# Autocorrelation on Trainium2: last-position terms and lag weights on ScalarE and GpSimd, a third key/value bank

## The chip, the cores and the metric

The kernel runs on one core of a Trainium2 chip. A core has five engines that execute their own instruction streams in order and synchronise by semaphores: TensorE (PE in the profile: matrix products and transposes), VectorE (DVE), ScalarE (ACT: functions, copies, scaling), GpSimd (POOL: element-wise work here) and SyncE (SP), which in this kernel issues nearly all DMA transfers. Matrix products accumulate in PSUM[...]; everything else lives in SBUF. A separate weight-load stream of TensorE is shown as PEld.

The metric is the device time in microseconds (us) of one execution. All data are fp32.

## The reference, cut to what matters

`x` and `ctx` have 8 batches of 256 positions and 1024 channels. Four layers follow one another:

```python
x = x + tanh(g_xattn[0]) * autocorrelation(layernorm(x), ctx, ctx)
x = x + tanh(g_ffn[0])   * lora_ffn(layernorm(x))
x = x + tanh(g_xattn[1]) * attention(layernorm(x), ctx, ctx, mask)   # GQA, rope
x = x + tanh(g_ffn[1])   * fourier_ffn(layernorm(x))
```

The change lies in the first of them. Per batch and channel:

```python
corr   = ifft(fft(q) * conj(fft(k))).real        # over L = 256 positions
w, idx = top_k(corr, 11)                         # 11 lags per channel
w      = softmax(w)
out    = sum_i w[i] * v[min(idx[i] + pos, L - 1)]
```

A shift beyond the end repeats the last position of `v`. So the sum over shifts is a linear correlation of the lag weights with `v`, in which the last position of `ctx` plays a part of its own.

## The kernel before, in words

The batches go in two passes of four. A pass p runs `autocorrelation`, then `lora_ffn`, `attention` and `fourier_ffn`, each with pools of its own. The program order is not written out by hand: the tile framework's scheduler orders the instructions from its own cost model, and inserts the semaphores; each engine then executes its list in order. Pools give a tile a new buffer when an old one has been released, so a pool with one buffer makes the next writer wait for the last reader.

**A turn.** `autocorrelation` works in turns: a turn is one batch and one half (512 channels) of D, 8 turns a pass, 16 in all. Positions are paired front and back, so a tile is 128 positions by 512 channels. In a turn:

- `loads`: DMA of the context `cn` and of its last position, `end`, spread over all partitions.
- `sums` (L460 to L466): GpSimd makes `ke`, `ko`, `qe`, `qo` (sums and differences of the pairs; L460 is `ke`). VectorE then corrects `ke` by -2 `end` (L466).
- `turn`: transforms by matmuls (`dft`, L411, into the pool `ps_dft`, four banks); ScalarE copies `kr`, `kn`, `ki`, `vr`, `vi` from PSUM to SBUF (L484 to L496); VectorE adds 2S `end` to row 0 of `kr` (L498). `products` (L427) multiplies spectra: four VectorE multiplications that read PSUM, two GpSimd sums for `re`, `im`.
- `correlation`: matmuls into the one bank of `ps_cor`, copied to `cor` by ScalarE.
- `lags`, four times a turn, each on 128 channels by 256 lags: VectorE finds the 8 largest and then three more, marking them by NEG (`match_replace`, L581 writes `took`); ScalarE computes `ex = exp(cor - max)` (L577); VectorE multiplies the mask `took == NEG` by `ex` and sums it into `tot` (L583); VectorE inverts `tot` (L586) and ScalarE scales `w` by it (L587).
- GpSimd makes `both`, the sums and differences of `w`'s halves.
- The next turn works up `both` of the turn before: TensorE transposes it into `pt` (pool `ps_out`, one bank; ScalarE copies it to `wt`), transforms `wt`, `products` with the spectra of `k` and `v` give `er`, `ei`, `odr`, `odi`, and `back` transforms them to positions (`po`, in `ps_dft`) and adds them to `x` by `residual` (L370, VectorE).

**What runs between.** At marked places a turn calls `fill(n)`, which advances a generator by n steps. That generator is `keys_values`: projections of the context to keys and values by a scheme of seven products instead of eight (`SEVEN`), matmuls at L796 into banks of the pool `ps_kv`, two of them. `combine` evicts a bank (VectorE; L244 is one of its lines). A finished key goes through `rope` (L709 to L717: three VectorE multiplications, the first two at L714 and L715 into a temporary of one buffer, and one GpSimd addition, L717). Weight sums for values and context sums run on GpSimd, those for keys on VectorE. In pass 0 `fold_last_layer` follows, which folds the last layer's update into its weight: matmuls at L319 into `ps_kv`, VectorE additions at L326. The same `rope` is called for queries in `attention`.

**PSUM in this stage.** Four banks `dft`, one `cor` (one tile of 128 x 512), one `out`, two `kv`: eight.

Of the kernel before, what the change touches and what calls it, by code (L numbers as in the profile page):

```python
# [11 lines left out]
F32 = mybir.dt.float32  # L12
# [7 lines left out]
P = 128  # L20
# [26 lines left out]
def flamingo_kernel(ctx: ExitStack, tc: tile.TileContext, a: dict, out: bass.AP):  # L47
# [333 lines left out]


    def autocorrelation(p, xt, pools, beside, late):
        c1, w1, w2, ps_dft, ps_cor, ps_out = pools

        def fill(n):
            for _ in range(n):
# [60 lines left out]
        def sums(b, cols, cn, end):  # L448

            xn = big_tile("xn", [2, HALF], "xn")  # L450
            for i, lin in enumerate(norms[b]):
                nc.scalar.activation(
                    xn[:, i, :],
                    xt[b * 2 + i][:, cols],
                    AF.Identity,
                    bias=lin[:, 1:2],
                    scale=lin[:, 0:1],
                )
            qe, qo, ke, ko = one("qe"), one("qo"), one("ke"), one("ko")
            nc.gpsimd.tensor_add(ke, cn[:, 0, :], cn[:, 1, :])  # L460
            nc.gpsimd.tensor_sub(ko, cn[:, 0, :], cn[:, 1, :])
            nc.gpsimd.tensor_add(qe, xn[:, 0, :], xn[:, 1, :])
            nc.gpsimd.tensor_sub(qo, xn[:, 0, :], xn[:, 1, :])


            nc.vector.scalar_tensor_tensor(ke, end, -2.0, ke, ALU.mult, ALU.add)  # L466
            return b, cols, end, qe, qo, ke, ko


# [2 lines left out]
        def turn(this, before, coming):  # L472


            after = None
            if this:
                b, cols, end, qe, qo, ke, ko = this
                if coming:
                    coming = loads(coming)
                kr_ps, ki_ps = dft((KCE, ke)), dft((KSE, ko), (NYQ, ke))  # L480


                kr, ki, kn = sb("kr"), sb("ki"), sb("kn")
                nc.scalar.copy(kr, kr_ps)  # L484
                nc.scalar.copy(kn, kr_ps)
                nc.scalar.activation(ki, ki_ps, AF.Copy, scale=pair)
                nc.scalar.copy(kn[0:1, :], ki_ps[0:1, :])
                re, im = sb("re"), sb("im")
                products(spectrum((CE, SE), (qe, qo)), kr, ki, kn, re, im, False)
                fill(2)  # L490

            if this:
                vr_ps, vi_ps = dft((KCO, ko)), dft((KSO, ke))
                vr, vi = sb("vr"), sb("vi")
                nc.scalar.copy(vr, vr_ps)
                nc.scalar.copy(vi, vi_ps)  # L496

                nc.vector.scalar_tensor_tensor(  # L498
                    kr[0:1, :], end[0:1, :], 2.0 * S, kr[0:1, :], ALU.mult, ALU.add
                )  # L500
                fill((1 if p == 0 else 2) if before else 6 if p == 0 else 2)
            last = not this
            if before:
                if last:
                    fill(3)
                b_cols, b_tiles, (bkr, bki, bkn, bvr, bvi, both) = before

                wt = []
                for t in range(2):
                    pt = ps_out.tile([P, HALF], F32, tag="out", name="pt")  # L510
                    for c in range(4):
                        nc.tensor.transpose(pt[:, c * P : (c + 1) * P], both[:, t, c, :], ident)
                    wt.append(one(f"wt{t}"))
                    nc.scalar.copy(wt[t], pt)
                    fill(2 if last else 1)
                er, ei = sb("re"), sb("im")
                products(spectrum((CE, SE), wt), bkr, bki, bkn, er, ei, True)
                fill(2 if last else 1)
                odr, odi = one("odr"), one("odi")
                products(spectrum((CO, SO), wt[::-1]), bvr, bvi, bvr, odr, odi, True)  # L520
                fill(3 if last else 2)
            if this and coming:
                after = sums(*coming)

            def back(l):


                if before:
                    po = ps_dft.tile([P, HALF], F32, tag="dft", name="po")
                    for i, (k, sp) in enumerate(((0, er), (3, odi)) if l else ((1, ei), (2, odr))):  # L530
                        nc.tensor.matmul(po, inv2[:, k, :], sp, start=(i == 0), stop=(i == 1))  # L531
                    residual(b_tiles[0][:, b_cols], po, tg_x[0])
                    residual(b_tiles[1][:, b_cols], po, tg_x[0] if l else ntg_x[0])
                    fill(1 - l)

            if last:
                back(0)
                back(1)
                return None, None
            w = big_tile("xn", [4, S], "w")  # L540
            cor = correlation(re, im, 0)
            fill(1)
            back(0)
            cor += correlation(re, im, 2)
            for c in range(2):
                lags(w[:, c, :], cor[c])
            fill(1)
            back(1)
            for c in range(2, 4):
                lags(w[:, c, :], cor[c])  # L550
            both = big_tile("xn", [2, 4, P], "both")
            nc.gpsimd.tensor_add(both[:, 0], w[:, :, 0:P], w[:, :, P:S])
            nc.gpsimd.tensor_sub(both[:, 1], w[:, :, 0:P], w[:, :, P:S])
            return after, (cols, xt[b * 2 : b * 2 + 2], (kr, ki, kn, vr, vi, both))
# [12 lines left out]
        def lags(w, cor):  # L567


            top = w2.tile([P, 16], F32, tag="top", name="top", bufs=4)  # L570
            left = w2.tile([P, S], F32, tag="left", name="left", bufs=1)
            took = w2.tile([P, S], F32, tag="took", name="took", bufs=1)
            nc.vector.max(top[:, 0:8], cor)
            neg = w2.tile([P, 1], F32, tag="neg", name="neg", bufs=4)
            nc.vector.tensor_scalar(neg, top[:, 0:1], -1.0, None, ALU.mult)
            ex = w2.tile([P, S], F32, tag="ex", name="ex")
            nc.scalar.activation(ex, cor, AF.Exp, bias=neg)  # L577
            nc.vector.match_replace(left, top[:, 0:8], cor, NEG)
            nc.vector.max(top[:, 8:16], left)
            nc.vector.memset(top[:, 11:16], NEG)  # L580
            nc.vector.match_replace(took, top[:, 8:16], left, NEG)  # L581
            tot = w2.tile([P, 1], F32, tag="tot", name="tot", bufs=4)
            nc.vector.scalar_tensor_tensor(  # L583
                w, took, NEG, ex, ALU.is_equal, ALU.mult, accum_out=tot
            )
            nc.vector.reciprocal(tot, tot)  # L586
            nc.scalar.activation(w, w, AF.Copy, scale=tot)  # L587

# [117 lines left out]
                pass  # L706


    def rope(dst, x, cos, sin, pool):  # L709

        H = P // 2
        t = pool.tile([P, 2, S], F32, tag="rope", name="rope", bufs=1)
        tab = lambda t: t.unsqueeze(1).to_broadcast([t.shape[0], 2, S])
        nc.vector.tensor_mul(t[0:H], x[H:P], tab(sin[H:P, :]))  # L714
        nc.vector.tensor_mul(t[H:P], x[0:H], tab(sin[0:H, :]))  # L715
        nc.vector.tensor_mul(dst, x, tab(cos))  # L716
        nc.gpsimd.tensor_add(dst, dst, t)  # L717

    def keys_values(n, groups, pools, tab):
# [61 lines left out]
        for u in range(4):  # L781
# [4 lines left out]
            for r in SEVEN:  # L786
# [16 lines left out]
                if done:  # L803
                    c, (i, j) = done
                    if kind == "wk":
                        kT = out_tile(c)
                        rope(kT, c, tab[:, 0, :], tab[:, 1, :], w1)
                        place = kT_d.rearrange("(q l i) p t -> q i p l t", l=2, i=2)
                        nc.sync.dma_start(
                            place[i_u, i, :, :, t0 + j * S : t0 + (j + 1) * S], kT  # L810
                        )
                    else:
                        r0, c0 = t0 + j * S, i_u * HALF + i * S
                        nc.sync.dma_start(
                            v_d[r0 : r0 + S, c0 : c0 + S].rearrange("(t p) d -> p t d", p=P), c
                        )
# [33 lines left out]
    def attention(p, xt, gq, go, keep, norms, xops, ahead):  # L850
        with (
# [115 lines left out]
            def queries(step, qT):  # L967
# [3 lines left out]
                for r in SEVEN:  # L971
# [10 lines left out]
                    done = combine(r, ps, tiles, lambda tag: half(tag, 1), lambda ps: ps)  # L982
                    if done:
                        qT[done[1]] = half("qT", 7)
                        rope(qT[done[1]], done[0], tab_q[:, 0, :], tab_q[:, 1, :], w1)
                    yield

            def outputs(step, ops):
# [359 lines left out]
    for p in range(NPASS):  # L1348
        ga, gb = ("a", "b") if p % 2 == 0 else ("b", "a")
        xt = [xpool.tile([P, D], F32, tag="x", name="x") for t in range(TT)]  # L1350
        with (
# [4 lines left out]
            tc.tile_pool(name="kv2", bufs=2, reuse_waits="tile") as kw2,  # L1356
            tc.tile_pool(name="ac_dft", bufs=4, space=PSUM) as ps_dft,
            tc.tile_pool(name="ac_cor", bufs=1, space=PSUM) as ps_cor,
            tc.tile_pool(name="ac_out", bufs=1, space=PSUM) as ps_out,
            tc.tile_pool(name="kv_ps", bufs=2, space=PSUM) as ps_kv,  # L1360
        ):

            tab = kw1.tile([P, 2, S], F32, name="tab")
# [15 lines left out]
            if p == 0:  # L1379
# [2 lines left out]
            autocorrelation(  # L1382
                p,
                xt,
                (c1, aw1, aw2, ps_dft, ps_cor, ps_out),
                steps,
                lambda: load_x(range(2, TT)),
            )
# [183 lines left out]
```

## Time and profile before

| | |
|---|---|
| three runs, us | 3363.13, 3356.34, 3361.8 |
| median, us | 3361.8 |
| profiled execution, us | 3351.35 |
| its span, first to last instruction, us | 3349.6 |
| mean granted TensorE clock | 0.992 |
| L466 (VectorE, `ke`), 16 times, ns least / median / most | 671 / 1215 / 6620 |
| L498 (VectorE, row of `kr`), 16 times | 716 / 1362 / 1697 |
| L583 (VectorE, `w`), 64 times | 403 / 425 / 7043 |
| L577 (ScalarE, exp), 64 times | 491 / 507 / 513 |
| L460 (GpSimd, `ke`), 16 times | 1251 / 1268 / 1457 |

The profile is one execution, and its own time differs a little from the runs. The span is what the trace covers. A busy engine is one that executes something; an engine is idle because it waits for a semaphore or has nothing to issue, and the trace names the instruction that released it. TensorE's clock is granted in parts of full speed, and the tables by stretches of time give its mean. Where a table of stretches is shown, each row has the stretch, its length, and then for every engine the busy time and the number of instructions. In a timeline a row has the start, the duration, engine, line and operation, and in brackets how long the engine stood idle before it and which instruction released it.

### The profile page before, as it was taken

The page shows a single profiled execution, that of the slowest core. Times are in us where ns is not written, and L with a number is a line of the kernel's source. Part 1 is how long each engine was busy: PE and PEld are TensorE (multiplying, and loading weights), DVE is VectorE, ACT ScalarE, POOL GpSimd, SP SyncE. Part 2 cuts the span into 40 slices and gives each one's busy share as a digit, 9 for nine tenths or more (in the row PEclk, how much of TensorE's full clock was granted, in tenths as well). Part 3 has the DMA queues.
Part 4 walks back from the last instruction along what each step waited for, and adds up shares of the span by engine and source line. Part 5 has one row for each costly group of instructions (what it writes and reads, how often), then busy time and mean ns, then how long its engine had stood idle before and what let it go on. Part 6 is the DMA issues. An engine that isn't in the chain of part 4 may idle for free. (4 is left out here: it accounts for less than half of the span.)

```text
span 3349.6 us, 39704 instructions
## 1 busy us (share of the span) xinstructions
PE 3268.8 (98%) x13456; PEld 2408.0 (72%) x13456; DVE 2356.0 (70%) x4561; ACT 844.1 (25%) x2043; POOL 1513.2 (45%) x1437
## 2 busy tenths in 40 slices
PE   8999899999999999999999999999999999999999
PEld 6677456777777766775456677568888888888874
DVE  7787657877777776776647686457776777777773
ACT  1332111322232322222113332113222223222310
POOL 4554112334433475576344442113464554554672
PEclk9999999999999999999999999999999999999999
DMA  7534615333333454554353435043555455555551
GB/s 280 174 113 125 240 59 189 127 136 132 139 126 129 132 207 147 178 190 160 116 189 127 141 120 166 7 159 101 166 182 161 157 168 175 164 168 172 176 186 51
DMA packets 215784, 505.58 MB, mean 151 GB/s; under 512 B 25076, under 2 KB 102900, under 8 KB 215582
## 3 DMA queue, kind: packets, MB, share of 16 engines
q1 hardware_dynamic: 214430, 498.84, 44.2%
q0 software_dynamic: 1152, 4.19, 0.3%
q8 instruction: 108, 1.77, 0.2%
q14 instruction: 94, 0.77, 0.1%
HBM read 394.96 MB, written 108.00 MB: 150 GB/s over the span
## 5 line engine op out<-in xcount | busy, mean ns | idle before, releaser
L717 POOL TENSOR_TENSOR qT<-qT,rope 128x512 f32<-128x512 f32 x128 | 169.3, 1322 | 671.0 <-DVE qT L716 670.9
L975 PE MATMUL ps_q<-xn,wq 128*128 128x256 f32 x1920 | 428.9, 379 | 0.0
L975 PEld LDWEIGHTS ps_q<-xn,wq 128*128 128x128 f32 x1920 | 364.8, 190 | 50.5 <-PE po L677 0.5
L1140 DVE COPY_PREDICATED s<-keep,ps_s 128x512 f32<-128x512 uint8 x256 | 185.5, 728 | 217.9 <-PE ps_s L1131 181.0
L1145 ACT ACTIVATE s<-s,nmx 128x256 f32<-128x256 f32 x512 | 255.9, 500 | 282.7 <-DVE nmx L1142 281.6
L975 PE MATMUL ps_q<-xn_t,wq 128*128 128x256 f32 x1280 | 285.6, 379 | 0.0
L1154 DVE TENSOR_SCALAR s<-s,tot 128x256 f32<-128x256 f32 x512 | 266.1, 560 | 7.5
L1172 ACT COPY wT<-pt 128x512 f32<-128x512 f32 x256 | 138.2, 588 | 526.8 <-PE pt L1166 526.3
L975 PEld LDWEIGHTS ps_q<-xn_t,wq 128*128 128x128 f32 x1280 | 243.2, 190 | 33.1
L370 DVE SCALAR_TENSOR_TENSOR x<-po,tg,x 128x512 f32<-128x512 f32 x248 | 176.4, 743 | 128.0 <-PE po L1319 45.7
L1177 PE MATMUL av<-wT,v 128*128 128x256 f32 x1024 | 246.0, 382 | 1.7 <-ACT wT L1172 1.4
L1131 PE MATMUL ps_s<-kT,qT 128*128 128x256 f32 x1024 | 247.5, 379 | 0.0
L1177 PEld LDWEIGHTS av<-wT,v 128*128 128x128 f32 x1024 | 191.6, 190 | 55.9 <-issue 21.5
L1067 PE MATMUL po<-wo,oI 128*128 128x256 f32 x896 | 215.7, 381 | 1.9 <-issue 1.2
L1131 PEld LDWEIGHTS ps_s<-kT,qT 128*128 128x128 f32 x1024 | 191.8, 190 | 25.5 <-issue 0.7
L1004 PE MATMUL po<-wo,oT 128*128 128x512 f32 x448 | 201.9, 593 | 0.0
L1139 POOL MEMSET s<- 128x512 f32 x256 | 128.7, 528 | 131.9 <-PE pt L1166 124.4
L1067 PEld LDWEIGHTS po<-wo,oI 128*128 128x128 f32 x896 | 169.8, 191 | 25.6 <-issue 1.8
L1142 DVE TENSOR_REDUCE nmx<-s 128x2 f32<-128x512 f32 x256 | 174.4, 684 | 7.7
L1067 PE MATMUL po<-wo,oT 128*128 128x256 f32 x672 | 171.7, 382 | 6.4 <-PE pt L1166 4.0
L253 POOL TENSOR_TENSOR x<-x,part 128x512 f32<-128x512 f32 x48 | 63.4, 1320 | 233.4 <-ACT part L252 233.4
L1185 ACT COPY oT<-av 128x512 f32<-128x512 f32 x128 | 75.0, 586 | 370.1 <-PE av L1177 370.1
(290 smaller groups left out, 6361.4 us busy)
## 6 DMA issues: line engine op xcount, KB each, us to landing
wo<-wo_d SPq DMA_DIRECT2D x144, 512.0 KB, 4.8
wq<-in_wq_dram SPq DMA_DIRECT2D x104, 512.0 KB, 3.5
wq<-wq_d SPq DMA_DIRECT2D x96, 512.0 KB, 3.3
wo<-in_wo_dram SPq DMA_DIRECT2D x56, 512.0 KB, 3.4
wo_d<-fine_t SPq DMA_DIRECT2D x56, 512.0 KB, 3.4
wo<-wo_d SPq DMA_DIRECT2D x96, 256.0 KB, 3.4
w<-w_d SPq DMA_DIRECT2D x36, 512.0 KB, 5.4
wo<-in_wo_dram SPq DMA_DIRECT2D x72, 256.0 KB, 3.3
```

Source lines behind the costliest of these rows:

```text
L370: nc.vector.scalar_tensor_tensor(xs, ps, g, xs, ALU.mult, ALU.add)
L717: nc.gpsimd.tensor_add(dst, dst, t)
L975: nc.tensor.matmul(ps[:, l, :], wops[r][:, l, c, :], xo[r][:, c, :], start=(c == 0), stop=(c == KH - 1),)
L1004: nc.tensor.matmul(po, ops[r][:, h, t * P : (t + 1) * P], wops[r][:, h, :], start=(h == 0), stop=(h == 1),)
L1067: nc.tensor.matmul(po, left[r2][:, h, :], w[:, h, :], start=(h == 0), stop=(h == 1))
L1131: nc.tensor.matmul(ps[:, t, :], qT[i, n][:, l, t * P : (t + 1) * P], kT[:, n * S : (n + 1) * S], start=True, stop=True,)
L1140: nc.vector.copy_predicated(s, keep[b], ps)
L1142: nc.vector.tensor_reduce(nmx, s, AX.X, ALU.max, negate=True)
L1145: nc.scalar.activation(s[:, t, :], s[:, t, :], AF.Exp, bias=nmx[:, t : t + 1], accum_out=tot[:, t : t + 1],)
L1154: nc.vector.tensor_scalar(s[:, t, :], s[:, t, :], tot[:, t : t + 1], None, ALU.mult)
L1172: nc.scalar.copy(wT[i], pt)
L1177: nc.tensor.matmul(av[:, i, :], kv[step][1][:, n * 2 + c, :], wT[i][:, c, :], start=(c == 0), stop=(c == 1),)
```

## The change

1. The correction of `ke` goes from one VectorE instruction to a ScalarE scaling of `end` by -2, in place, and a GpSimd addition.
2. The correction of row 0 of `kr` goes from one VectorE instruction to a ScalarE scaling of the already scaled row (-S times -2 `end` is 2S `end`) into a new tile `back_end`, and a GpSimd addition on one partition.
3. In `lags`, the masked product with its sum is replaced. ScalarE exponentiates `took`, in which the chosen lags stand as NEG and become zero, and the 16 values of `top`, of which the last five are NEG, with their sum as `tot`. GpSimd subtracts: `w = ex - exp(took)`, which leaves the chosen lags. `took` gets two buffers instead of one (the pool's number).
4. `pt` moves to the pool `ps_dft`. The pool `ps_out` goes, and `ps_kv` has three banks instead of two.
5. `rope` takes the number of buffers of its temporary as an argument: two for keys, one, as before, for queries.

```diff
-        c1, w1, w2, ps_dft, ps_cor, ps_out = pools
+        c1, w1, w2, ps_dft, ps_cor = pools
...
-            nc.vector.scalar_tensor_tensor(ke, end, -2.0, ke, ALU.mult, ALU.add)
+            nc.scalar.activation(end, end, AF.Copy, scale=-2.0)
+            nc.gpsimd.tensor_add(ke, ke, end)
...
-                nc.vector.scalar_tensor_tensor(
-                    kr[0:1, :], end[0:1, :], 2.0 * S, kr[0:1, :], ALU.mult, ALU.add
-                )
+                back_end = one("back_end")
+                nc.scalar.activation(back_end[0:1, :], end[0:1, :], AF.Copy, scale=-1.0 * S)
+                nc.gpsimd.tensor_add(kr[0:1, :], kr[0:1, :], back_end[0:1, :])
...
-                    pt = ps_out.tile([P, HALF], F32, tag="out", name="pt")
+                    pt = ps_dft.tile([P, HALF], F32, tag="dft", name="pt")
...
-            took = w2.tile([P, S], F32, tag="took", name="took", bufs=1)
+            took = w2.tile([P, S], F32, tag="took", name="took")
...
             tot = w2.tile([P, 1], F32, tag="tot", name="tot", bufs=4)
-            nc.vector.scalar_tensor_tensor(
-                w, took, NEG, ex, ALU.is_equal, ALU.mult, accum_out=tot
-            )
+            nc.scalar.activation(took, took, AF.Exp, bias=neg)
+            nc.scalar.activation(top, top, AF.Exp, bias=neg, accum_out=tot)
+            nc.gpsimd.tensor_sub(w, ex, took)
             nc.vector.reciprocal(tot, tot)
             nc.scalar.activation(w, w, AF.Copy, scale=tot)
...
-    def rope(dst, x, cos, sin, pool):
+    def rope(dst, x, cos, sin, pool, bufs):
...
-        t = pool.tile([P, 2, S], F32, tag="rope", name="rope", bufs=1)
+        t = pool.tile([P, 2, S], F32, tag="rope", name="rope", bufs=bufs)
...
-                        rope(kT, c, tab[:, 0, :], tab[:, 1, :], w1)
+                        rope(kT, c, tab[:, 0, :], tab[:, 1, :], w1, 2)
...
-                        rope(qT[done[1]], done[0], tab_q[:, 0, :], tab_q[:, 1, :], w1)
+                        rope(qT[done[1]], done[0], tab_q[:, 0, :], tab_q[:, 1, :], w1, 1)
...
-            tc.tile_pool(name="ac_out", bufs=1, space=PSUM) as ps_out,
-            tc.tile_pool(name="kv_ps", bufs=2, space=PSUM) as ps_kv,
+            tc.tile_pool(name="kv_ps", bufs=3, space=PSUM) as ps_kv,
```

More of the change, by code (lines that the diff above doesn't have):

```diff
@@ L1384, in flamingo_kernel @@
                 xt,
-                (c1, aw1, aw2, ps_dft, ps_cor, ps_out),
+                (c1, aw1, aw2, ps_dft, ps_cor),
                 steps,
```

## The prediction

> **What bounds the kernel now.** First the page's busy times: TensorE (PE) is occupied 98% of the span. Then busy time by stage. The change lies in the two autocorrelation stages, 0 to 374 us and 1720 to 2080 us, and in the fold behind the first.
>
> ```profile
> span 3349.6 us, 39704 instructions
> PE 3268.8 (98%) x13456; PEld 2408.0 (72%) x13456; DVE 2356.0 (70%) x4561; ACT 844.1 (25%) x2043; POOL 1513.2 (45%) x1437
> ...
> 0.00:374.00 374.00, 352.80 (x1355) 256.18 (x1356) 274.52 (x667) 102.70 (x182) 181.02 (x149) 0.98 0.51 174
> 374.00:480.00 106.00, 95.05 (x327) 48.74 (x326) 75.02 (x170) 11.16 (x23) 10.79 (x8) 0.97 0.48 169
> 1720.00:2080.00 360.00, 341.34 (x1335) 250.53 (x1334) 255.99 (x629) 96.95 (x174) 164.56 (x129) 0.98 0.44 145
> ```
>
> The columns are length, then PE, weight loads, VectorE (DVE), ScalarE (ACT), GpSimd (POOL), clock, DMA. PE is the bound here too; only its idle time can be won: 21.2 us in the first stage, 18.7 in the second. Added to that is the time it runs at half clock after a long gap:
>
> ```profile
> 75.60:82.40 6.80, 4.75 (x11) 3.87 (x12) 5.20 (x11) 0.77 (x1) 6.37 (x5) 0.50 0.31 117
> 130.20:133.60 3.40, 3.40 (x7) 2.02 (x8) 3.26 (x11) 1.48 (x3) 0.37 (x1) 0.51 0.00 0
> 1737.90:1744.70 6.80, 5.69 (x14) 4.55 (x15) 4.68 (x12) 0.30 (x1) 1.27 (x1) 0.50 0.48 134
> 1789.10:1792.50 3.40, 3.40 (x7) 2.04 (x7) 2.01 (x4) 0.00 (x0) 2.34 (x3) 0.50 0.63 193
> 1908.60:1915.40 6.80, 2.90 (x7) 2.37 (x8) 6.80 (x8) 0.00 (x0) 2.59 (x3) 0.50 0.53 176
> ```
>
> Last, who makes PE wait: the source view of line 466, and the timeline around the longest gap.
>
> ```profile
> L466 DVE SCALAR_TENSOR_TENSOR ke<-end,ke x16: 671/1215/6620, 26.0 to 1987.1; 128x512 f32<-128x512 f32 x16
> ...
>   POOL ke L460: 66.1, 15
> ...
> 1904.62 6.62 DVE L466 SCALAR_TENSOR_TENSOR ke<-end,ke 128x512 f32<-128x512 f32 x1 [7.98 <-POOL ke L460]
> ...
> 1912.50 0.80 PE L796 MATMUL ps_k<-cx,wk 128*128 128x256 f32 x1 [6.35 <-DVE v L244]
> ...
> 114.37 7.04 DVE L583 SCALAR_TENSOR_TENSOR w<-took,ex 128x256 f32<-128x256 f32 x1
> ```
>
> VectorE stands at L466 for GpSimd's ke (66.1 us over 15 turns), then spends 6.62 us on an operation that costs 0.67 at best. The evictions of the key and value banks queue behind it, and PE, with two such banks, stops.
>
> **The change, part by part.** A turn is one (batch, half) step; there are 16, each with four lags.
>
> *VectorE loses* L466, L498 and L583. From their minima and excess over them: 16 x 0.67 + 13.6 = 24.3; 16 x 0.72 + 7.8 = 19.3; 64 x 0.40 + 9.5 = 35.3, and 64 accumulator reads of 0.083 = 5.3. Together 84 us, with 66 us of standing.
>
> *GpSimd gains* two additions a turn and one subtraction a lag. 128x512 costs 1.27 (L460), 128x256 0.73 (L1046); one row of 512 I take at 1.27 too, since time goes by row length (ScalarE's one-row copy L487 takes 0.56 against 0.59): 32 x 1.27 + 64 x 0.73 = 87 us. Its stages go from 345.6 to some 433 of 734 us: room on the mean, but it executes in order.
>
> *ScalarE gains*, per lag, exp of 128x256 (0.50, L577) and exp of 128x16 (0.30, L350's small row) with accumulator read (0.19, L1145); per turn the scaling (0.6 as L484) and a row (0.56): 64 x 0.99 + 16 x 1.16 = 82 us on 200 of 734. The order of instructions has 24 function-table loads before and after.
>
> *What is won on PE.* Gaps with this cause, each with the half clock behind it (half of the stretches above):
> - 73.2: 4.10 + 3.4. The rope at L714 waits 6.37 for L717's addition, which stands behind GpSimd's weight sums; the second rope buffer and third bank remove it.
> - 124.5: 5.02 + 1.7. The residual L370 is behind the 7.04 us L583.
> - 217.6 and 277.6: 1.1 + 0.7 (bank behind L466; residual late).
> - 1734.1 and 1784.0: 4.52 + 3.4 and 3.62 + 1.7, evictions behind L466.
> - 1822.4: 1.80, GpSimd's re behind ko; in the new order PE has other work there.
> - 1905.6: 6.35 + 3.4.
> Sum 40.8 us.
>
> *What the next thing in line takes back.* At 73.2 PE comes 7.5 us early to the key transform, 77.8 instead of 85.3. GpSimd ended ko at 80.3 and the new addition ends at 81.6, the rope addition now behind it: 3.8 back. At 124.5 ScalarE's multiplication by 1/tot must wait for GpSimd's subtraction, queued behind weight sums up to 118.65 for the first lag and 121.9 for the second. Behind it in ScalarE's order stand the second exp and the second cor copy (end 123.8 instead of 122.9). Through the lags the residual ends at 128.2 instead of 129.95: PE still waits 3.3 + 1.7, 5.0 back. At 1734.1 and 1784.0 I take back 1 each, for the later ke. At 1905.6, from both at 1895.4, GpSimd has some 19 operations to the end of odr, 1919.4; PE would need it at 1924.4 - 9.75 = 1914.6: 4.8, and some half clock, 5.8 back. Together 16.6; 24.2 us stay.
>
> *New waits.* A lag's end loses the VectorE product (0.43 + 0.08) and gets exp, exp-with-sum and subtraction; after the match_replace it is about 0.7 us later, and recip on VectorE now waits for ScalarE where it followed at once. Behind recip stand the next lags and the residuals that free PE's transform bank; in turns at 167, 203, 241, 314 and 1852 they end 0.4 to 1.0 us before PE needs them. I take 0.3 for 12 turns, 3.6. Where PE already waits for both without slack (353.5 and 2051.7) 1.1 each; in the turn at 152, two table loads of 1.28 now lie before the last exp: 0.7. Together 6.5. Nothing (a gain in VectorE time alone) would be below these; 3 us per turn above.
>
> *pt in the transform banks:* it follows the spectrum products; they end 1.7 to 5 us before pt in most turns: nothing, or 0.5 a turn if ScalarE's copies come late. *Loads:* as many as before; the end loads shift on SP by a few places among weights that no PE wait names. *Fold:* 14 products now come in a row; VectorE (0.6 per 128x512, by their starts) sets the pace. It reaches the last additions, which free the next stage's banks, at 401.5 instead of 403.65, and the weight loads behind them shift alike: 2.4 won.
>
> Net: 24.2 - 6.5 + 2.4 = 20 us. The profiled execution took 3351.35 (span 3349.6 and 1.75 around it) and becomes 3331; from the median of 3361.8, 3341.5.
>
> **Two rules weighed.** *Gap and clock.* The row: after gaps of 4.10, 4.52 and 6.35 us half clock held for 6.8 us, after 5.02 and 3.62 for 3.4. [...] I take the row. [...] Left are those reading PSUM (L370 0.74, L427 0.68) and one-input ones (L581 0.41, L348 0.67), which keep their durations beside a busy GpSimd: no charge.
>
> **Rivals.**
> 1. *Nearly all is kept*: ScalarE and GpSimd are prompt, so only the wait for ke at 73.2 comes back: 40.8 - 3.8 - 2 + 2.4 = 37; 3325. For it: ScalarE 27% busy, GpSimd idle some 10 us ahead of most both. Against: in-order queues.
> 2. *No change*: gaps move. New waits of 1.5 us a turn (24) eat the 24.2: 3360. For it: PE stands close behind the residuals.
> 3. *Slower: the lag loop VectorE, ScalarE, GpSimd.* ScalarE stands at L587's scaling for a subtraction; behind it wait the copies of kr and ki, so the products, so the banks. Price: 3 us in each of 16 turns, 48 us, less 26.6 won, plus half clock of 1.7 in a few: +25, 3387. It decides from 1.7 us a turn on. For it: in two turns GpSimd's sums stand in the way. Against: in the other turns GpSimd is idle then.
> 4. *VectorE was not the cause* and PE waits for the cor/lag chain itself[...]; 3352.
>
> **How the numbers follow.** Forecast 0.55, rival 1 0.10, rival 4 0.08, rival 2 0.13, rival 3 0.14. The runs before lie within 0.2%, 6.7 us: that is what a measurement tells from no change. Faster takes the forecast, 1 and 4, less 0.02 of tails: 0.71; same 0.14; slower 0.15. The likeliest one's own range is 3330 to 3354. The range takes in rivals 1 and 2 and the mild half of 3: 3322 to 3373; outside is about 0.15.
>
> **What would show it.** VectorE about 84 us less in all, POOL +87, ACT +80. In the stages PE idle from 40 to about 25. No PE wait over 4 us at 73, 1734 and 1784; one left of some 3 us near 124 on L370; near 1905 one on GpSimd's odr. If ScalarE's line 587 waits for POOL w by more than 2 us in most turns, rival 3 holds; if PE's idle time in the stages stays at 40, the cause was elsewhere.

## The result, and the profile after

The changed kernel takes 3386.68 us (median of 4 runs, 3383.54 to 3390.19); the kernel before, 3362.47. The ratio is 1.0082, 95% interval 1.0068 to 1.0096: slower by 24 us, where 20 us faster was forecast. The time lies above the range of the prediction.

The page of the changed kernel and its busy times in stretches of the two stages (second stage shifted, since it begins 15 us later; columns as in the prediction):

```profile
span 3384.8 us, 39881 instructions
PE 3278.7 (97%) x13456; PEld 2414.0 (71%) x13456; DVE 2292.9 (68%) x4401; ACT 905.2 (27%) x2267; POOL 1590.6 (47%) x1533
...
0.00:374.00 374.00, 351.19 (x1355) 255.34 (x1356) 242.17 (x587) 133.14 (x294) 220.29 (x197) 0.99 0.50 174
1735.00:2104.00 369.00, 333.81 (x1280) 243.53 (x1279) 213.25 (x540) 127.54 (x286) 199.80 (x175) 0.94 0.39 131
```

The work moved about as forecast: VectorE 63 us less, ScalarE 61 more, GpSimd 77 more. TensorE gained nothing: in the first stage its busy time is what it was, in the second it is idle for 35 us of 369, and its clock there is 0.94 instead of 0.98.

To place the loss I take the start times of six matmuls by their number in TensorE's order, which hardly differs between the kernels: the first, those numbered 1370 (in the fold), 1500 (in the next layer), 6340 (some 33 us ahead of the second stage), 7560 (near its end), and the last. Two executions were profiled of each kernel; the second of each is the control described with the experiments.

| us between these matmuls | before | before, again | after | after, again |
|---|---|---|---|---|
| first stage | 375.3 | 376.2 | 374.8 | 374.6 |
| fold and head of the next layer | 45.2 | 45.1 | 48.8 | 48.4 |
| attention and the last layer, first pass | 1260.4 | 1258.7 | 1272.1 | 1270.0 |
| second stage | 346.2 | 338.7 | 369.4 | 371.9 |
| rest | 1310.8 | 1308.9 | 1308.3 | 1311.4 |

On the mean of two, 28 us are lost in the second stage, 11.5 in attention, 3.4 in the fold; 1 is won in the first stage. That is 42 us and not 24, because the two profiled executions of the kernel before are faster than its medians (3351.35 and 3341.27 against 3362.47 and 3356.88): what its slower executions lose more no profile here shows, so the split holds for the profiled executions, the ratio for the time.

Who makes TensorE wait in the second stage of the changed kernel (the waits by engine and line: total, times, longest):

```profile
PE dft L411 <- ACT wt L515: 28.0, 4, 8.9
PE dft L411 <- ACT kn L486: 4.2, 1, 4.2
PE pt L513 <- POOL both L553: 1.8, 1, 1.8
```

None of the waits of the kernel before is there (1734, 1784, 1822, 1905; such numbers give, as in the prediction, the start of the last matmul ahead of a wait). A new one is: four times TensorE stands for ScalarE's copy of `pt`. The wait of 4.2 us for `kn` has the same origin: ScalarE has stood for a load until 1777.86, and the lag instructions behind it come ahead of the copy of `kn`. The timeline of one of the four, ScalarE first, then the DMA queue (SPq), GpSimd and TensorE:

```profile
1842.82 0.57 ACT L515 COPY wt<-pt 128x512 f32<-128x512 f32 x1
1851.36 0.63 ACT L466 ACTIVATE end<-end 128x512 f32<-128x512 f32 x1 [7.97 <-DMA end<-in_ctx_dram]
1851.89 0.57 ACT L515 COPY wt<-pt 128x512 f32<-128x512 f32 x1
...
1845.65 0.33 SPq L445 DMA_DIRECT2D end<-in_ctx_dram  x1
...
1844.36 1.27 POOL L467 TENSOR_TENSOR ke<-ke,end 128x512 f32<-128x512 f32 x1
...
1844.48 1.02 PE L411 MATMUL dft<-wt,mats 128*128 128x512 f32 x2
1852.52 2.08 PE L411 MATMUL dft<-wt,mats 128*128 128x512 f32 x2 [7.01 <-ACT wt L515]
```

Between its two copies of `pt` ScalarE scales `end` by -2, for the addition that comes two turns later, and stands 7.97 us for the load. The load is no sooner because `end` has two buffers: it is issued at 1845.65, when GpSimd's addition of two turns before (L467, to 1845.6) has released one. So the chain runs GpSimd's addition, load (5.3 us at the median), ScalarE's scaling, the copy behind it, TensorE. The source view of the load, before and after, says it in one line each. Before, nobody waits for it:

```profile
L445 SPq DMA_DIRECT2D end<-in_ctx_dram x16: 333/418/1108, 16.3 to 1948.8; - x16
...
who waited for it (us, times):
```

After, ScalarE does in 14 of 16 turns:

```profile
L445 SPq DMA_DIRECT2D end<-in_ctx_dram x16: 328/402/822, 16.9 to 1941.7; - x16
...
who waited for it (us, times):
  ACT end L466: 99.1, 14
```

With each of these five gaps comes a stretch at half clock, which begins while TensorE still stands; three of the five are longer than any row that the prediction took (stretches of the changed kernel; the clock is the third column from the end):

```profile
1783.10:1789.90 6.80, 5.03 (x8) 2.68 (x9) 5.56 (x21) 5.54 (x15) 2.73 (x3) 0.50 0.35 116
1800.10:1810.30 10.20, 5.96 (x11) 3.87 (x12) 1.29 (x2) 2.52 (x4) 3.86 (x4) 0.50 0.47 171
1847.90:1858.10 10.20, 5.58 (x11) 3.84 (x12) 1.29 (x2) 2.52 (x4) 2.74 (x3) 0.50 0.56 171
1895.70:1902.50 6.80, 3.31 (x6) 2.01 (x7) 1.20 (x2) 3.00 (x5) 0.42 (x1) 0.50 0.81 286
1943.50:1953.70 10.20, 5.76 (x11) 3.87 (x12) 1.29 (x2) 2.52 (x4) 5.63 (x5) 0.50 0.52 179
```

That is 44 us at half clock, in which TensorE is busy for 25.6. In the timeline above two matmuls of L411 take 2.08 us in such a stretch and 1.02 ahead of it, so by an estimate from these about half of the 25.6, 13 us, is lost beside the 32 us of waits.

Why only the second stage? ScalarE stands for the load in the first as well (44.4 us in 6 waits). What differs is the place of L466 in ScalarE's order. In the second stage it stands, in four turns, between the two copies of `pt`, as in the timeline above: L515, L466, L515. In the first stage it stands behind both copies of a turn, or ahead of the first turns. ScalarE stands 9.50 us there ahead of the scaling at 150.02, and TensorE runs on without a gap.

### The profile page after: what moved, and what is told of

The parts are those of the page before. It is cut to its first block, busy times and chain, and to the rows that moved or that the text cites. A ratio compares the mean times of both kernels' runs of the same rounds, so it can differ in the third digit from the quotient of the medians.

```text
span 3384.8 us, 39881 instructions
## 1 busy us (share of the span) xinstructions
PE 3278.7 (97%) x13456; PEld 2414.0 (71%) x13456; DVE 2292.9 (68%) x4401; ACT 905.2 (27%) x2267; POOL 1590.6 (47%) x1533
## 4 chain that ended last, share of the span: by engine, by line
PE 80%; DVE 6%; POOL 5%; DMA 3%; issue 2%; ACT 1%; SPq 0%; POOLq 0%; DVEq 0%; ACTq 0%
PE ps_q L977 22%; PE po L1069 9%; PE po L1006 9%; PE av L1179 6%; PE ps_s L1133 6%; PE po L670 6%; PE po L1321 5%; PE ps_k L798 3%; PE pt L1168 3%; PE dft L411 3%; PE ps_v L798 3%; DVE s L1156 1%; DMA end<-in_ctx_dram 1%; PE po L532 1%; PE pa L626 1%
## 5 line engine op out<-in xcount | busy, mean ns | idle before, releaser
L1156 DVE TENSOR_SCALAR s<-s,tot 128x256 f32<-128x256 f32 x512 | 272.2, 572 | 7.5
L1144 DVE TENSOR_REDUCE nmx<-s 128x2 f32<-128x512 f32 x256 | 174.5, 684 | 7.7
```

The source lines that it names most:

```text
L1144: nc.vector.tensor_reduce(nmx, s, AX.X, ALU.max, negate=True)
L1156: nc.vector.tensor_scalar(s[:, t, :], s[:, t, :], tot[:, t : t + 1], None, ALU.mult)
```

## Experiments

Theories: S, ScalarE stands in order for the load of `end`, and TensorE for what is queued behind; L, the lag loop over VectorE, ScalarE and GpSimd (the prediction's third rival); A, the loss comes from attention, where VectorE is held. Ratios are to the kernel before, on the same chip. Four columns give the profile's segments as above, and "held" counts the places in attention and the last layer of the first pass where VectorE's scaling of the weights (L1154 before, L1156 after) takes over 2.5 us instead of 0.35.

| | ratio, 95% interval | first stage | fold | attention, last layer | second stage | held |
|---|---|---|---|---|---|---|
| after | 1.0082 (1.0068 to 1.0096) | 374.8 | 48.8 | 1272.1 | 369.4 | 5 |
| L466 in program order | 0.9932 (0.9912 to 0.9953) | 376.7 | 48.6 | 1270.2 | 322.5 | 5 |
| L466 and L500 in program order | 0.9943 (0.9925 to 0.9962) | 377.3 | 50.1 | 1270.1 | 322.5 | 5 |
| after, lags on VectorE | 1.0044 (1.0028 to 1.0059) | 374.6 | 49.2 | 1270.1 | 365.0 | 5 |
| both in order, lags on VectorE | 0.9940 (0.9922 to 0.9957) | 372.8 | 50.9 | 1259.4 | 322.7 | 2 |
| after, `ke` and `kr` on VectorE | 0.9957 (0.9942 to 0.9973) | 377.1 | 49.7 | 1269.7 | 327.7 | 5 |
| before + `ke` | 1.0023 (1.0011 to 1.0035) | 376.5 | 45.1 | 1262.1 | 351.7 | 3 |
| before + `ke` in program order | 0.9951 (0.9931 to 0.9970) | 377.6 | 45.1 | 1265.8 | 324.8 | 4 |
| before + bank, rope buffers | 0.9941 (0.9924 to 0.9958) | 366.4 | 51.1 | 1267.4 | 327.4 | 5 |
| before + bank, rope, `ke` in order | 0.9940 (0.9925 to 0.9955) | 376.0 | 48.5 | 1269.5 | 322.7 | 5 |
| before + lags | 1.0018 (1.0006 to 1.0030) | 381.3 | 45.3 | 1262.3 | 338.5 | 3 |

**One scheduling edge.** The same instructions on the same engines; L466 may only not be issued ahead of what the program names before it on ScalarE, and comes to stand behind L452 of its own turn, starting 1.4 us after it in most turns, instead of as much as two turns ahead (the expectation says nearly one).

```diff
-            nc.scalar.activation(end, end, AF.Copy, scale=-2.0)
+            tc.keep_in_program_order(nc.scalar.activation(end, end, AF.Copy, scale=-2.0))
```

> The changed kernel with one scheduling edge more: ScalarE's scaling of end (L466) may not be issued ahead of what the program names before it on ScalarE, so it moves from nearly a turn early to behind the same turn's normalisation L452. Same instructions, same engines. Theory S (ScalarE stands in order for the end load, 99.1 us in 14 waits, and the copies wt of L515 queue behind it): the wait at L466 falls from 99 to under 15 us, the four TensorE waits for L515 in the second stage (28.0 us and their half clock) go, and the time falls by about 23 us to 3355 to 3370. Rival L (lag loop: ScalarE's L589 waits for GpSimd's subtraction): nothing changes, 3380 to 3390. Rival A (the loss lies in attention, where VectorE's L1156 is starved 8 us at a time, 11 of the 24 us): only what the phase gives, 3375 to 3395.

Measured: 3338.28 us, 48 less than the changed kernel, 0.68% faster than the kernel before. The source view of L466 and TensorE's longest waits in the second stage:

```profile
L466 ACT ACTIVATE end<-end x16: 612/614/633, 27.6 to 1981.3; 128x512 f32<-128x512 f32 x16
...
  DMA end<-in_ctx_dram: 8.6, 3
```

```profile
PE pt L513 <- POOL both L553: 1.8, 1, 1.8
PE ps_k L798 <- DVE x L370: 0.8, 1, 0.8
PE pt L365 <- DVE xn L355: 0.6, 1, 0.6
```

The wait for the load fell from 99.1 to 8.6 us, the four waits are gone, and the second stage is 46.9 us shorter; no other segment moved by more than 2. TensorE's order is the same in both kernels, matmul for matmul. This is what theory S forecast, at twice the price that was expected: the expectation counted back to the kernel before, but behind the wait lay the gain of the change, too. Theory A falls as the cause; the loss in attention stays all the same, 1270.2 us here, too.

**The second edge.** L500 held in the same way, `tc.keep_in_program_order(nc.scalar.activation(back_end ...))`. In the changed kernel it stands 41.7 us for GpSimd's L501.

> As the run with L466 held in program order, and the scaling of the row into back_end (L500) held as well, so it stands behind the copy of vi. Theory S: beside the wait for end, the 41.7 us that ScalarE stands at L500 for GpSimd's L501 go too; 0 to 8 us below the run with one edge, 3350 to 3365. Rival L: 3380 to 3390. Rival A: 3375 to 3395.

The ratios overlap, 0.9943 and 0.9932, and the second stage takes 322.5 in both. The expectation held that up to 8 us lay in the 41.7. This run cannot tell, since the first edge had removed them already: with L466 held alone, the scheduler places L500 directly behind it, and ScalarE does not stand at L500 at all. So the first edge took two waits of ScalarE away at once. Which of them counted is told by the timeline, in which TensorE is released by the copy behind L466, and by a pair of kernels without L500, the `ke` correction alone, further down.

**The lags.** In the changed kernel, `lags` as before:

```diff
-            nc.scalar.activation(took, took, AF.Exp, bias=neg)
-            nc.scalar.activation(top, top, AF.Exp, bias=neg, accum_out=tot)
-            nc.gpsimd.tensor_sub(w, ex, took)
+            nc.vector.scalar_tensor_tensor(
+                w, took, NEG, ex, ALU.is_equal, ALU.mult, accum_out=tot
+            )
```

> The changed kernel with the lags as before: VectorE's masked product with its sum is back, ScalarE's two exponentials and GpSimd's subtraction are out, took has one buffer. Theory S: ScalarE still stands at L466 for the end load, 80 to 100 us, TensorE still waits at L515 in the second stage; 3375 to 3392. Rival L: the loss is gone, 3340 to 3360.

It stays slower than before, with ScalarE standing 81.4 us for the load in 12 waits and TensorE 26.4 us for the copies. Theory L falls as the cause of the loss, though not wholly: the intervals of 1.0044 and 1.0082 do not overlap, so the lags part adds 0.4% here. How much of that comes by way of the load's wait, 81.4 us against 99.1, is not told apart. The same edit with both edges:

> The changed kernel with L466 and L500 held in program order and the lags back on VectorE with one buffer of took. It tells what the lags part is worth once ScalarE no longer stands for the load: 3338 to 3344 if it is worth nothing, 3345 to 3358 if VectorE's masked product costs TensorE its waits again (0.4 us in each of 64 lags and the held ones).

0.9940 against 0.9943: once the wait is gone, no worth of the lags part, for better or worse, can be told. Alone on the kernel before:

> The kernel before with the lags alone on ScalarE and GpSimd (two exponentials, the subtraction, two buffers of took). By the prediction's sum of new waits and of the 124.5 gap, between 6 us slower and 6 us faster; 3353 to 3368. Rival L (lag loop): 3375 or more. Places with 8 us of held VectorE in attention: 2 if the banks bring the others.

1.0018, slightly slower. The profile shows 5.5 us more in the first stage than the mean of the two of before, and in the second the time of the faster of the two profiles of before. In the first stage TensorE's wait at 174.9 for `both` is new (2.6 us), that at 357.7 is 2.5 (1.4 before), that at 281.9 is 1.2 (0.7 before).

**Both corrections back on VectorE.** The changed kernel with L466 and L498 of the kernel before.

> The changed kernel with both corrections by end back on VectorE, so ScalarE reads end nowhere; lags on ScalarE and GpSimd, third bank, two rope buffers stay. Theory S: no wait of ScalarE for a load, no TensorE wait for L515 over 4 us; VectorE stands for ke again; 3345 to 3365. Rival L: 3380 to 3395. Rival A: 3370 to 3395.

0.9957: ScalarE never stands for the load of `end`, and there is no wait for L515 over 4 us. So the two corrections, as they were placed, cost the changed kernel 1.25%.

**The `ke` correction alone**, on the kernel before:

```diff
-            nc.vector.scalar_tensor_tensor(ke, end, -2.0, ke, ALU.mult, ALU.add)
+            nc.scalar.activation(end, end, AF.Copy, scale=-2.0)
+            nc.gpsimd.tensor_add(ke, ke, end)
```

> The kernel before with the first part alone: ScalarE scales end by -2 (L466), GpSimd adds it to ke; the row of kr stays on VectorE, with a factor that fits the scaled end. Theory S: ScalarE is given the scaling early and stands for the end load, 80 to 110 us in all, TensorE waits for the copies wt behind it in the second stage; slower than before by 10 to 35 us, 3372 to 3397. Rival (the third bank or the lags make the change slow): 3345 to 3365. In attention, VectorE is held for 8 us at a time in 2 places as in the kernel before if the banks bring the other places, in 4 or 5 if any change of the stage does.

1.0023, less than was expected. The wait is there, 56.7 us in 12 places, and TensorE stands three times for the copies, 13.1 us in all; in ScalarE's list L466 lies between two copies of `pt` in three turns, where it was four in the changed kernel. With the edge:

> The kernel before with the first part alone, as run earlier, but ScalarE's scaling of end (L466) held in program order. Theory S: the wait of ScalarE for the end load (56.7 us in 12 waits when not held) and the waits of TensorE for the copies wt in the second stage (5.9, 2.6 and 4.6 us) go; the ratio to the kernel before falls from 1.0023 to 0.992 to 0.999. If the part is slow for another reason (GpSimd's addition late), it stays at 1.000 to 1.004.

0.9951, the wait 9.4 us in 3 places, none of TensorE for L515. The lines, first without the edge, then, behind the mark, with it:

```profile
ACT end L466 <- DMA end<-in_ctx_dram: 56.7, 12, 8.9
PE dft L411 <- ACT wt L515: 13.1, 3, 5.9
...
ACT end L466 <- DMA end<-in_ctx_dram: 9.4, 3, 4.9
```

In this pair TensorE and VectorE execute the same order; ScalarE's L466 and, with it, GpSimd's L467 are all that moved. Here theory S is shown without the second wait beside it. So the same edit is worth plus 0.2% or minus 0.5%, by the place of one instruction.

**The third bank and the rope buffers alone**, on the kernel before (parts 4 and 5 of the diff):

> The kernel before with the third key/value bank, pt in the transform banks and two rope buffers, nothing else. If the banks bring the new order of the fold: the fold and the head of the next layer take about 3 us more, attention of the first pass has 4 or 5 places where VectorE is held for 8 us, which costs 10 us; the stages win 5 to 15; together 3352 to 3368. If they do not, 2 such places and 3345 to 3358.

0.9941, better than expected: both stages gain (9.4 us in the first, 15 in the second against the mean of two). TensorE's waits at 1734 and 1784 are gone, that at 73.2 is 1.7 us instead of 4.1, although VectorE stands 72.8 us for `ke`, longer than before. I take it that with a bank more the evictions behind it have time; the bank, the move of `pt` and the rope buffers were not run apart. The fold loses 6 us. There VectorE stands 7.55 us with a residual ahead of the weight sums (the timeline of this kernel):

```profile
410.40 0.75 DVE L370 SCALAR_TENSOR_TENSOR x<-po,tg,x 128x512 f32<-128x512 f32 x1 [7.55 <-PE po L677]
411.06 2.35 DVE L141 TENSOR_TENSOR w_t<-w,w 128x1024 f32<-128x1024 f32 x2
```

In the kernel before, L141 is issued at 415.39 ahead of that residual. In the kernel with the bank TensorE waits 3.8 us for L141's result, as in the changed kernel; before, 0.8.

**A candidate** from these: bank, rope buffers, `ke` with the edge; the row of `kr` and the lags on VectorE.

> A candidate: third key/value bank, pt in the transform banks, two rope buffers, the ke correction on ScalarE and GpSimd with L466 held in program order; the row of kr and the lags stay on VectorE. If the parts add: the first stage as with the banks alone (9 us shorter than before), the second as with both edges (24 us shorter), ratio to before 0.989 to 0.993; if not, 0.993 to 0.996.

0.9940: the parts do not add. The second stage is as with the edges, but the first loses what the bank alone had won (376.0 against 366.4). VectorE's masked product of the lags is held there for 8.3 and 3.9 us, at 114 and 159. The six kernels from 0.9932 to 0.9951 are not told apart by their intervals; each of them beats both kernels of this case.

**Controls.** Both kernels once more, for a second profile.

> The kernel before once more, for a second profile. If the loss of 11 us between the fold and the second pass in the profile of the changed kernel is chance of the execution, this one has more than two places in attention where VectorE's scaling (L1154) is held for 8 us, and takes more than 1260.4 us between those two points; if it belongs to the change, two places and 1259 to 1262 us.

> The changed kernel once more, for a second profile. Chance: another number of held places than four of 8 us and one of 3.4 us; belonging to the change: the same five. The four TensorE waits for L515 in the second stage stay in both cases, 20 us and more in all.

The kernel before shows no held place this time, where both branches of its expectation had two or more, and takes 1258.7 us where it took 1260.4; the changed kernel shows the same five, and the four waits for L515 (32.4 us). So the five are no chance of one execution. The segment's time goes with their number: 1258.7 to 1260.4 us with none to two, 1262 to 1266 with three or four, 1267 to 1272 with five. In the changed kernel four of the five are each followed by a wait of TensorE of 2.9 to 4.2 us, 13.3 in all; in the first profile of the kernel before, two make 7.0. The places are not bound to one part either: nine profiled executions have the third bank, and eight of them show five, one (both in order, lags on VectorE) two; the five without it show 0 to 4. One of them in the timeline of the changed kernel, VectorE's, then GpSimd's, then TensorE's rows:

```profile
1468.94 8.32 DVE L1156 TENSOR_SCALAR s<-s,tot 128x256 f32<-128x256 f32 x2
...
1468.20 1.26 POOL L262 TENSOR_TENSOR x<-x,part 128x512 f32<-128x512 f32 x1
1469.43 1.26 POOL L261 TENSOR_TENSOR x<-x,part 128x512 f32<-128x512 f32 x1
...
1474.36 1.27 POOL L923 TENSOR_TENSOR fine_t<-wo 128x512 f32<-128x512 f32 x1
1475.58 1.27 POOL L926 TENSOR_TENSOR fine_t<-fine_t,wo 128x512 f32<-128x512 f32 x1
1479.31 1.29 POOL L924 TENSOR_TENSOR fine_t<-wo,wo 128x512 f32<-128x512 f32 x1 [2.46 <-DMA wo_d<-fine_t]
...
1478.70 3.24 PE L1006 MATMUL po<-wo,oS 128*128 128x512 f32 x4 [3.37 <-DVE x L370]
```

VectorE begins while GpSimd works; its first operation takes 8.06 us and ends, at 1477.00, just after GpSimd's unbroken run of element-wise operations, which ends at 1476.85. The residual behind it is late, and TensorE stands 3.4 us. Which offset between the two engines brings this about, and why the kernels with the bank fall into it, stays open.

## Why the prediction was wrong, point by point

**The step that failed** is "ScalarE gains": the scaling of `end` was entered by its duration alone, "the scaling (0.6 as L484)", as part of 82 us "on 200 of 734", and under *Loads* the prediction said that the end loads shift "among weights that no PE wait names". The duration was right (0.63). What was left out is the wait that the moved instruction takes with it. On VectorE the same load was waited for by an instruction that already stood 66 us for GpSimd, so it never showed in a wait. On ScalarE the scaling needs nothing but the load, and it was placed about two turns early (the scaling at 1851.36 serves the addition L467 at 1940.46), in front of copies that TensorE needs: ScalarE stood 99.1 us for the load, and TensorE 28.0 us for the copies. The edge that moves it back, and L500 with it, turns 1.0082 into 0.9932; with the `ke` part alone, where there is no L500, it turns 1.0023 into 0.9951. Why the scheduler placed it so early is not on record. The list of new waits has entries for VectorE, GpSimd and table loads, but none for a DMA.

**The rest of the sum.** With that wait gone the kernel takes 3338.3 us; 3341.5 was forecast. That agreement is partly luck. By segments this kernel is only 4 us shorter than the mean of the two profiles of before (the fold is 3.4 longer and attention 10.7, neither of which was forecast), while by the medians it is 24 shorter. Its second stage is 20.0 us shorter than the mean of the two profiles of before, against 14 in the forecast (24.8 won, 7.8 taken back, 2.9 of new waits): the wait at 1905 left nothing behind, where 5.8 had been entered. But that wait, the largest item of the sum, belonged to one execution: in the second profile of the kernel before VectorE's L466 takes 1.74 us at this place instead of 6.62, and TensorE waits 1.45 instead of 6.35. These are its rows:

```profile
1902.82 1.74 DVE L466 SCALAR_TENSOR_TENSOR ke<-end,ke 128x512 f32<-128x512 f32 x1 [7.97 <-POOL ke L460]
...
1905.81 1.56 PE L796 MATMUL ps_k<-cx,wk 128*128 128x256 f32 x6 [1.45 <-DVE v L244]
```

The first stage of the kernel with the edge is 0.9 longer, against 3.6 shorter. There, the gap at 73.2 shrank to 0.7 us at 79.3 (3.8 had been entered) and the wait for `both` at 354.0 grew by the 1.1 entered; but the residual at 121.3 costs 5.5 (3.3 entered), `both` at 174.5 costs 2.7 (0.7 entered), and a wait of 2.2 us for weight sums at 41.6 is new.

**The fold** was to win 2.4 and lost 3.4. TensorE was released by the last addition at 402.6 instead of 403.7; what was missed is VectorE's order behind them, the residual ahead of L141.

**Attention** was not mentioned, and has 11.5 us of the profiled difference. The prediction charged nothing for one-input VectorE operations beside a busy GpSimd, because L581 and L348 kept their durations (402 to 411 ns and 627 to 696 ns). The row that spoke against it was in the trace of before, one input from SBUF, 353 ns at the median and 8016 at most:

```profile
L1154 DVE TENSOR_SCALAR s<-s,tot x512: 333/353/8016, 579.1 to 3187.5; 128x256 f32<-128x256 f32 x171
```

The trace shows how long such an operation took and which GpSimd operations ran beside it; why it took so long no run shows.

**The rivals.** Rival 3 named 3387, the measured time, for another reason. Its sign was to be L587's wait by more than 2 us in most turns; ScalarE stood there (L589 in the changed kernel) 29.8 us in 22 of 64 lags, and 28.7 us in 23 of 64 in the faster kernel with the edge. A wait of the same size in both explains no difference. What the lags part adds to the changed kernel, 0.4% by the run with the lags on VectorE, is a part of the loss and far from the 48 us that the rival priced. Rival 4, that VectorE was not the cause, falls: the bank with the rope buffers, and the `ke` correction with its edge, each take most of the second stage's waits.

**Signs.** POOL +77 (87 forecast), ACT +61 (82), VectorE -63 (84; L1154 alone took 6.1 more, 272.2 for 266.1). Unit costs were right (L467 1.27, L501 1.26, L587 0.74, L585 0.51, L586 0.29 and 0.19); busy time counts a moment in which two instructions of an engine overlap once, and the durations alone add up to 81 us more on ScalarE. TensorE's wait at 109.25 on `odr` (3.6 us) came in the first stage and not at 1905.

**Half clock.** The prediction entered half of each stretch at half clock. But three of its five rows begin while TensorE still stands: in 1908.60:1915.40 it starts again at 1912.50 and is busy for 2.90 of the 6.80 us. Half of the busy times, (4.75 + 3.40 + 5.69 + 3.40 + 2.90) / 2, is 10.1 us, where 13.6 was entered: these entries were 3.5 us too large in all, which is not what made the forecast wrong. Nor does a gap alone tell the length. In the second profile of the kernel before, the gap of 4.54 us at 1734 had 3.4 us of half clock, where one of 4.52 had 6.8:

```profile
1739.20:1742.60 3.40, 3.40 (x10) 2.69 (x9) 2.73 (x9) 0.30 (x1) 0.39 (x1) 0.50 0.47 120
```

In the changed kernel gaps of 6.36, 7.01 and 8.92 us had 10.2, those of 4.21 and 5.70 had 6.8; in its second profile gaps of 6.18, 6.88 and 8.85 us had 6.8.

## What to carry to other kernels

When an instruction goes to another engine, list all that it waits for, loads too, and then read in the new engine's order what stands behind it: a wait hidden under a longer one on the old engine can come out on the new, as here: VectorE stood 66.1 us for `ke` and none for the load, ScalarE 99.1 us for the load. An instruction whose only input is a load may be placed far ahead by the scheduler, as L466 was, up to 89 us ahead of the addition that it serves; where the buffer of that load is released late, hold the instruction in program order. When such an edge is tried, read what else moved with it: here a second wait went as well, and it took another pair of kernels to tell the two apart. And a part's worth is not fixed: with the place of one instruction it went from 0.5% faster to 0.2% slower.

## What the runs showed of the hardware

In the changed kernel GpSimd's addition on one row of 512 took as long as that on 128 rows (medians of 16: L501 1.258 us, L467 1.265). There a VectorE scaling with one SBUF input, L1156, 0.353 us at the median, took up to 8.06 us, over seven successive GpSimd operations of 1.26 to 1.28 us, and ended at GpSimd's first pause (2.46 us). The five stretches at half clock in its second stage began inside TensorE's gaps of 4.21 to 8.92 us. The lengths of such stretches differed between executions of one kernel: in the two profiles of the kernel before, gaps of 4.52 and 4.54 us had 6.8 and 3.4 us.
